# Four graph layers on one core: the tile pools' waits go from "all users of the space" to "users of the tile's own bytes"

## The chip, the cores and the metric

The kernel runs on one core of a Trainium2 chip. A core has five engines that each work off their own queue in order: TensorE (PE, with its weight loads shown as PEld), VectorE (DVE), ScalarE (ACT), GpSimd (POOL) and SyncE (SP, which here only starts transfers). They meet through semaphores: an instruction carries a list of waits and starts when all are met. Transfers run on 16 DMA engines and are started from the queues of SP, ACT and POOL. The metric is the device time of one execution in microseconds (us); less is better.

## The reference

A batch of N = 4096 nodes with D = 128 features and a dense adjacency matrix `adj` of 4096 by 4096 in float32 (64 MB). `adj` holds zeros and ones, is symmetric, and has ones on its diagonal. Four layers follow each other, each as `x = layernorm(x + layer(x, adj))`:

```python
# layer 0: hyperbolic GNN; pairwise weights times log maps
adj_att = adj * jax.nn.sigmoid((x_tangent @ wl)[:, None] + (x_tangent @ wr)[None, :] + att_b[0])
support_t = jnp.einsum('ij,ijd->id', adj_att, x_local)      # x_local[i, j] = logmap(h_i, h_j)
out = proj(expmap0(proj(expmap(h, support_t))))
# layer 1: transformer convolution, 4 heads of 32
e = jnp.where(mask[None], 0.0, jnp.exp(neg - m))            # mask = (adj == 0)
out = jnp.einsum('hnm,mhc->hnc', e / denom, v)              # then a learned gate against x @ Ws + bs
# layer 2: graph convolution with adj + I, normalised by degree
out = jax.nn.relu((d[:, None] * (adj + I) * d[None, :]) @ x @ weight)
# layer 3: additive attention over the neighbours
e = leaky_relu(A * s + A * r.T, 0.2)
out = softmax(where(A > 0, e, NEG), axis=1) @ (X @ W.T + b)
```

## The kernel before, in words

`tile_kernel` runs the program twice in source, once on the chip. First comes the class `Fast`, which relies on properties of the inputs (zeros and ones, symmetry, small scores) and checks them as it goes. It leaves flags in `good`. Only if a flag is bad does the class `Net`, from which `Fast` inherits, run again in full under `tc.If(again > 0)`. With these inputs it does not run, so the profile shows `Fast` alone.

`Fast` works in blocks of 512 by 512 (8 by 8 blocks of `adj`), each made of 4 tiles of 128 rows.

- **Layer 0, preparation** (0 to 75 us): the node vectors, norms and row constants. Its pools are closed by `pre_pools.close()`.
- **Layer 0, `pair_loop`** (75 to 646 us): 36 pairs of blocks (I, J) with I not above J, in an order written out by hand. For each pair PE makes the products `pz` (L1775 and L1778), ACT the sigmoids `w` (L1792) and the logarithms and exponentials, DVE the products, and PE the sums `pi` (L1859) and `pj` (L1874), which DVE adds into `X` (L1888). SP loads the float32 blocks `ad` and the row constants `di` and `dj`; POOL loads `el` and `er` and writes a bfloat16 copy of every block, `adjb`, to DRAM.
- **Layer 0, `mirror`** (646 to 745 us): a check that `adjb` is symmetric. SP loads 36 blocks `low` (L1683) and 28 blocks `up` (L1686), 512 KB each, into three buffers of each kind. PE multiplies them by the small matrices `sized` (made on DVE, L1677) and adds 12 steps into one PSUM tile `pm` (L1692, L1697; two buffers). DVE reduces each such sum to one column of flags, `odd` (L1702). In the same stretch DVE, ACT and POOL compute the end of layer 0: the `junk` sums (L537 and L541) and what follows to L604.
- **Layer 1, start** (745 to 790 us): ACT's queue loads the first block for the attention, `at0` (L2166). PE transposes `X` (L163), ACT and DVE copy the transposes out (L178), PE makes queries and keys (`pqk`, L2201), ACT and DVE cut them into two parts `cut` (L2203, L2204), SP stores these to DRAM as `qk` (L2210), and POOL loads them from there stacked by head, as `KS` and `QS` (L2181). Values (L2216) and `x @ Ws + bs` (L2226) follow on PE.
- **Layer 1, `attention_unshifted`** (790 to 1590 us): scores on PE (`ps`, L1994), exponentials on ACT (L2001, after a table load), mask on DVE (`e`, L2003), sums over neighbours on PE (`pv`, L2020). Beside it ACT's queue loads rows of `adj` (`nat`, L1970) and ACT sums them to degrees (L1976). SP loads the blocks `at` (L1959). At the end DVE normalises `X` (L2078, then L2094).
- **`layers23`** (1590 to 2048 us): layer 2 splits the features `Y` into three bfloat16 parts (ACT L2353, DVE L2355) and multiplies them by the blocks from `ring` on PE (`pa`, L2372). Meanwhile SP loads rows of `adj` (`nat`, L2331) that DVE looks through for values other than zero and one (L2336). Layer 3 follows in `attend_factored` (DVE L1570, PE L1573).

Pools are opened and closed by stage: `tc.tile_pool(name=..., bufs=...)` takes a stretch of SBUF or PSUM, and a later stage's pool lies on bytes that an earlier one gave back. The first tile in such reused bytes has to wait for their earlier users. By default a pool does that as a whole: its first tile waits for all the users of the closed pools that it lies on, in lists of up to some 18 semaphores. The order within each engine comes from the order in the source, and in parts from a list written out by hand (`pair_loop`).

Of the kernel before, what the change touches and what calls it, by code (L numbers as in the profile page):

```python
# [9 lines left out]
F32 = mybir.dt.float32  # L10
F32R = mybir.dt.float32r
BF16 = mybir.dt.bfloat16
# [3 lines left out]
PSUM = bass.MemoryType.PSUM  # L16

P = 128
# [43 lines left out]
class Net:  # L62
# [30 lines left out]

    def copies(self):
        self.adjT = self.dram.tile([self.NS, self.NS, P, 4, S], F32, tag="adjT", name="adjT")

    def pools(self, ctx, adj, big, t, o):

        self.on_scalar = 4
        if adj:  # L100
            self.adjp = ctx.enter_context(self.tc.tile_pool(name="adjp", bufs=adj))
        if big:
            self.ps_big = ctx.enter_context(self.tc.tile_pool(name="ps_big", bufs=big, space=PSUM))
        self.ps_t = ctx.enter_context(self.tc.tile_pool(name="ps_t", bufs=t, space=PSUM))
        self.ps_o = ctx.enter_context(self.tc.tile_pool(name="ps_o", bufs=o, space=PSUM))
# [202 lines left out]
    def layer0(self, x, weight, bias, att_w, att_b):  # L308
# [4 lines left out]
        with ExitStack() as ctx:  # L313
            self.on_scalar = 4
            keep = ctx.enter_context(tc.tile_pool(name="keep0", bufs=1))
            self.cols = ctx.enter_context(tc.tile_pool(name="cols0", bufs=1))
            adp = ctx.enter_context(tc.tile_pool(name="ad0", bufs=2))
            pre_pools = ctx.enter_context(ExitStack())
            pre = pre_pools.enter_context(tc.tile_pool(name="pre0", bufs=2))
            self.ps_t = pre_pools.enter_context(tc.tile_pool(name="ps_t", bufs=6, space=PSUM))  # L320
            one = pre_pools.enter_context(tc.tile_pool(name="one0", bufs=1))
            self.wide = pre_pools.enter_context(tc.tile_pool(name="wide", bufs=1))
            ps_c = pre_pools.enter_context(tc.tile_pool(name="ps_c", bufs=1, space=PSUM))
# [187 lines left out]
            late = ctx.enter_context(tc.tile_pool(name="late0", bufs=1))  # L511
            rot = ctx.enter_context(tc.tile_pool(name="rot0", bufs=6))
# [92 lines left out]
    def pair_loop(self, HT, HA, dr, rows, adp, early, rows4):  # L605
# [7 lines left out]
        with ExitStack() as ctx:  # L613
            atp = ctx.enter_context(tc.tile_pool(name="at0", bufs=2))
            wtp = ctx.enter_context(tc.tile_pool(name="sg0", bufs=6))
            wk = ctx.enter_context(tc.tile_pool(name="wk0", bufs=2))
            ps_t = ctx.enter_context(tc.tile_pool(name="ps_t0", bufs=2, space=PSUM))
            ps_z = ctx.enter_context(tc.tile_pool(name="ps_z0", bufs=2, space=PSUM))
            ps_i = ctx.enter_context(tc.tile_pool(name="ps_i0", bufs=1, space=PSUM))
            ps_j = ctx.enter_context(tc.tile_pool(name="ps_j0", bufs=1, space=PSUM))  # L620
# [224 lines left out]
    def layer1(self, Wq, bq, Wk, bk, Wv, bv, Ws, bs, Wb, R):  # L845
# [6 lines left out]
        with ExitStack() as ctx:  # L852
            self.on_scalar = 4
            keep = ctx.enter_context(tc.tile_pool(name="keep1", bufs=1))
# [27 lines left out]
            with ExitStack() as pctx:  # L882
                pre = pctx.enter_context(tc.tile_pool(name="pre1", bufs=1))
                rot = pctx.enter_context(tc.tile_pool(name="rot1", bufs=2))
                self.ps_t = pctx.enter_context(tc.tile_pool(name="ps_t", bufs=8, space=PSUM))
# [59 lines left out]
    def attention_unshifted(self, VA, KS, QS, at0, stack, R, wb):  # L945
# [4 lines left out]
        with ExitStack() as ctx:  # L950
            rot = ctx.enter_context(tc.tile_pool(name="rotf", bufs=1))
            natp = ctx.enter_context(tc.tile_pool(name="natf", bufs=2))
            atp = ctx.enter_context(tc.tile_pool(name="atf", bufs=1))
            ep = ctx.enter_context(tc.tile_pool(name="ef", bufs=3))
            ps_s = ctx.enter_context(tc.tile_pool(name="ps_s", bufs=3, space=PSUM))
            ps_v = ctx.enter_context(tc.tile_pool(name="ps_v", bufs=1, space=PSUM))
# [198 lines left out]
    def attention_shifted(self, V, qk, R, wb, spare):  # L1155
# [4 lines left out]
        with ExitStack() as ctx:  # L1160
            self.pools(ctx, 1, 2, 3, 1)
            self.wide = ctx.enter_context(tc.tile_pool(name="wide", bufs=2))
            keep = ctx.enter_context(tc.tile_pool(name="keeps", bufs=1))
            self.cols = ctx.enter_context(tc.tile_pool(name="cols1", bufs=1))
# [12 lines left out]
            work = ctx.enter_context(tc.tile_pool(name="work1", bufs=1))  # L1177
# [98 lines left out]
    def layers23(self, w2, weight, bias, a_s, a_r, out, Y):  # L1276
# [6 lines left out]
        with ExitStack() as ctx:  # L1283
            RING = 8
            ring = ctx.enter_context(tc.tile_pool(name="ring", bufs=1)).tile([P, RING, 4, S], F32, tag="ring", name="ring")
            keep = ctx.enter_context(tc.tile_pool(name="keep3", bufs=1))
# [10 lines left out]
            pre = pctx.enter_context(tc.tile_pool(name="pre3", bufs=1))  # L1297
            rot = pctx.enter_context(tc.tile_pool(name="rot2", bufs=2))
            wp = pctx.enter_context(tc.tile_pool(name="w2", bufs=4))
            ps_b = pctx.enter_context(tc.tile_pool(name="ps_b", bufs=2, space=PSUM))  # L1300
            ps_t = pctx.enter_context(tc.tile_pool(name="ps_t", bufs=2, space=PSUM))
            ps_s = pctx.enter_context(tc.tile_pool(name="ps_s", bufs=2, space=PSUM))
            ps_a = pctx.enter_context(tc.tile_pool(name="ps_a", bufs=2, space=PSUM))
# [228 lines left out]
    def attend_factored(self, F, XB, rho, col, wx, tot, eps, a0, ring, out):  # L1532
        nc, tc, N, NT, NS, D, X = self.nc, self.tc, self.N, self.NT, self.NS, self.D, self.X
        with ExitStack() as ctx:
            rot = ctx.enter_context(tc.tile_pool(name="rot3", bufs=2))
            RING = ring.shape[1]
            wp = ctx.enter_context(tc.tile_pool(name="w3", bufs=4))
            ps_a = ctx.enter_context(tc.tile_pool(name="ps_a3", bufs=2, space=PSUM))
            ps_b = ctx.enter_context(tc.tile_pool(name="ps_b3", bufs=2, space=PSUM))
# [43 lines left out]
    def attend(self, H, Rb, ring, weight, br, a_s, a_r, out):  # L1583
        nc, tc, N, NT, D, X = self.nc, self.tc, self.N, self.NT, self.D, self.X
        with ExitStack() as ctx:
            self.pools(ctx, 0, 0, 6, 2)
            self.wide = ctx.enter_context(tc.tile_pool(name="wide", bufs=2))
            one = ctx.enter_context(tc.tile_pool(name="one3", bufs=1))
            self.cols = ctx.enter_context(tc.tile_pool(name="cols3", bufs=1))
# [4 lines left out]
            with tc.tile_pool(name="pre3", bufs=1) as pre:  # L1594
# [15 lines left out]
            work = ctx.enter_context(tc.tile_pool(name="work3", bufs=1))  # L1610
# [33 lines left out]
class Fast(Net):  # L1644

    MARKS = 112

# [16 lines left out]
    def mirror(self, ctx):  # L1664
# [3 lines left out]
        keep = ctx.enter_context(tc.tile_pool(name="mir", bufs=1))  # L1668
        rot = ctx.enter_context(tc.tile_pool(name="mirt", bufs=3))
        ps = ctx.enter_context(tc.tile_pool(name="mirp", bufs=2, space=PSUM))  # L1670
# [38 lines left out]
    def pair_loop(self, HT, HA, dr, rows, adp, early, rows4):  # L1709
# [7 lines left out]
        with ExitStack() as ctx:  # L1717
            wtp = ctx.enter_context(tc.tile_pool(name="sg0", bufs=6))
            wk = ctx.enter_context(tc.tile_pool(name="wk0", bufs=2))
            ps_z = ctx.enter_context(tc.tile_pool(name="ps_z0", bufs=4, space=PSUM))  # L1720
            ps_i = ctx.enter_context(tc.tile_pool(name="ps_i0", bufs=1, space=PSUM))
            ps_j = ctx.enter_context(tc.tile_pool(name="ps_j0", bufs=1, space=PSUM))
# [218 lines left out]
    def attention_unshifted(self, VA, KS, QS, at0, stack, R, wb):  # L1941
# [4 lines left out]
        with ExitStack() as ctx:  # L1946
            rot = ctx.enter_context(tc.tile_pool(name="rotf", bufs=1))
            natp = ctx.enter_context(tc.tile_pool(name="natf", bufs=2))
            atp = ctx.enter_context(tc.tile_pool(name="atf", bufs=1))
            ep = ctx.enter_context(tc.tile_pool(name="ef", bufs=3))  # L1950
            ps_s = ctx.enter_context(tc.tile_pool(name="ps_s", bufs=3, space=PSUM))
            ps_v = ctx.enter_context(tc.tile_pool(name="ps_v", bufs=1, space=PSUM))
# [197 lines left out]
    def layer1(self, Wq, bq, Wk, bk, Wv, bv, Ws, bs, Wb, R):  # L2150
# [6 lines left out]
        with ExitStack() as ctx:  # L2157
            self.on_scalar = 4
            keep = ctx.enter_context(tc.tile_pool(name="keep1", bufs=1))
# [26 lines left out]
            with ExitStack() as pctx:  # L2186
                pre = pctx.enter_context(tc.tile_pool(name="pre1", bufs=1))
                rot = pctx.enter_context(tc.tile_pool(name="rot1", bufs=2))
                self.ps_t = pctx.enter_context(tc.tile_pool(name="ps_t", bufs=8, space=PSUM))
# [55 lines left out]
    def layers23(self, w2, weight, bias, a_s, a_r, out, Y):  # L2245
# [6 lines left out]
        with ExitStack() as ctx:  # L2252
            RING = 8
            ring = ctx.enter_context(tc.tile_pool(name="ring", bufs=1)).tile([P, RING, 4, S], BF16, tag="ring", name="ring")
            keep = ctx.enter_context(tc.tile_pool(name="keep3", bufs=1))
# [9 lines left out]
            pre = pctx.enter_context(tc.tile_pool(name="pre3", bufs=1))  # L2265
            rot = pctx.enter_context(tc.tile_pool(name="rot2", bufs=2))
            wp = pctx.enter_context(tc.tile_pool(name="w2", bufs=4))
            ps_b = pctx.enter_context(tc.tile_pool(name="ps_b", bufs=2, space=PSUM))
            ps_t = pctx.enter_context(tc.tile_pool(name="ps_t", bufs=2, space=PSUM))
            ps_s = pctx.enter_context(tc.tile_pool(name="ps_s", bufs=2, space=PSUM))  # L2270
            ps_a = pctx.enter_context(tc.tile_pool(name="ps_a", bufs=2, space=PSUM))
            parts = [pre.tile([P, NT, D], BF16, tag=f"Y{k}", name=f"Y{k}") for k in range(3)]
            identb = pre.tile([P, P], BF16, tag="identb", name="identb")
            nc.vector.tensor_copy(identb, self.ident)
            w = self.load_mat(w2, "w2")
            br = self.load_row(bias, "br3", keep)
            wn = self.load_mat(weight, "wn3", pre)
# [301 lines left out]
```

## Time and profile before

| | before |
|---|---|
| time, median of 3 runs | 2050.09 us (2048.27 to 2053.14) |
| profiled execution | 2050.21 us |
| its span in the profile | 2048.4 us |
| mean granted TensorE clock | 0.954 of full speed |
| busy: PE, DVE, ACT, POOL | 1900.9, 1736.6, 1328.8, 171.4 us |
| moved by DMA | 350.22 MB, mean 171 GB/s |

The span runs from the first to the last instruction of the profiled execution; 1.8 us lie around it. Busy times are sums over the whole span: an engine with a high sum can still be waiting at the start of a stage. The chain in the profile is the work that ended last, followed back from the end, at each step to what released it. Line numbers (L1683) are those of the kernel before.

### The profile page before, as it was taken

Reading aid. Unit: us, or ns where it says so; the run is one execution under the profiler, and the core shown is the slowest. Engines: PE = TensorE matmul, PEld = TensorE weight load, DVE = VectorE, ACT = ScalarE, POOL = GpSimd, SP = SyncE. Lnnn points to the kernel's source line nnn. Section 1 sums busy time; section 2 is a strip of 40 time slices with the busy share of each in tenths; the row PEclk is TensorE's granted clock in tenths of the full one; section 3 lists DMA queues with packets and bytes.
Section 4 is the critical chain, followed back from the end, with each engine's and each line's share of the span. In section 5 each row is a group of like instructions: output and inputs, shape, how many; then the busy total and the mean of one; then the engine's idle time right before and its main releaser. Section 6 shows DMA issues by size and latency. Waiting matters only on the chain.

```text
span 2048.4 us, 23818 instructions
## 1 busy us (share of the span) xinstructions
PE 1900.9 (93%) x8648; PEld 978.9 (48%) x8680; DVE 1736.6 (85%) x2685; ACT 1328.8 (65%) x1681; POOL 171.4 (8%) x269
## 2 busy tenths in 40 slices
PE   4789999999997788999999999999999799999997
PEld 4257766666666454333333333333333344444443
DVE  6579999998988946789999999999999777778986
ACT  5589999999997723777787777778787322210000
POOL 2211112111100221300000000000000000000000
PEclk8569999999999998999999999999999999999999
DMA  3488989899825977853535453545343799934441
GB/s 101 49 139 147 155 167 157 155 163 168 144 93 191 363 277 223 199 152 132 144 124 146 136 150 134 144 133 155 124 139 118 290 396 373 340 116 156 155 148 43
DMA packets 138064, 350.22 MB, mean 171 GB/s; under 512 B 13196, under 2 KB 56364, under 8 KB 125648
## 3 DMA queue, kind: packets, MB, share of 16 engines
q1 hardware_dynamic: 82944, 230.27, 32.3%
q0 software_dynamic: 45632, 50.69, 20.1%
q10 hardware_dynamic: 9360, 67.64, 9.9%
q8 instruction: 70, 1.15, 0.2%
q14 instruction: 58, 0.48, 0.1%
HBM read 371.54 MB, written 44.12 MB: 203 GB/s over the span
## 4 chain that ended last, share of the span: by engine, by line
PE 49%; DVE 24%; ACT 16%; DMA 6%; issue 4%; SPq 0%; POOL 0%; another core or an unknown queue 0%; ACTq 0%; DVEq 0%; POOLq 0%
PE pv L2020 11%; PE pa L1573 9%; DVE e L2003 9%; PE pa L2372 7%; PE ps L1994 6%; ACT e L2001 4%; PE pz L1775 3%; DMA up<-adjb 3%; DVE nat L1985 2%; ACT w L1792 2%; PE pi L1859 2%; PE pj L1874 2%; ACT s L1815 2%; ACT y L1811 2%; ACT y L1807 1%
## 5 line engine op out<-in xcount | busy, mean ns | idle before, releaser
L2003 DVE SCALAR_TENSOR_TENSOR e<-at,e 128x2048 f32<-128x2048 bf16 x256 | 582.6, 2286 | 77.3 <-ACT e L2001 76.7
L2001 ACT ACTIVATE e<-ps 128x1024 f32<-128x1024 f32 x512 | 492.9, 1024 | 150.6 <-PE ps L1994 121.6
L2020 PE MATMUL pv<-e,VA 128*64 128x512 f32 x2048 | 497.6, 607 | 6.7 <-DVE e L2003 5.7
L1994 PE MATMUL ps<-QS,KS 128*128 128x512 f32 x1024 | 314.8, 425 | 9.1 <-ACT e L2001 8.5
L1994 PEld LDWEIGHTS ps<-QS,KS 128*128 128x128 f32 x1024 | 170.9, 189 | 236.5 <-ACT e L2001 177.4
L2020 PEld LDWEIGHTS pv<-e,VA 128*64 128x64 f32 x2048 | 125.1, 136 | 250.2 <-issue 214.4
L1573 PE MATMUL pa<-w,Y 128*128 128x512 f32 x448 | 195.3, 594 | 0.0
L1775 PE MATMUL pz<-HT 128*128 128x512 f32 x288 | 171.8, 681 | 15.0 <-DVE w L1847 10.2
L1570 DVE SCALAR_TENSOR_TENSOR w<-rho,col,ring 128x512 f32<-128x512 f32 x224 | 162.7, 746 | 22.3 <-PE pa L1573 9.7
L2372 PE MATMUL pa<-ring,Y 128*128 128x512 bf16 x750 | 172.7, 384 | 8.7 <-ACT Y L2353 6.7
L1859 PE MATMUL pi<-HA,w 128*128 128x129 f32 x1152 | 156.6, 286 | 6.5 <-ACT s L1815 5.3
L1859 PEld LDWEIGHTS pi<-HA,w 128*128 128x128 f32 x1152 | 143.3, 199 | 18.2 <-issue 10.2
L1573 PEld LDWEIGHTS pa<-w,Y 128*128 128x128 f32 x448 | 83.8, 190 | 105.9 <-issue 80.3
L1976 ACT ACTIVATE nat<-nat 128x2048 f32<-128x2048 f32 x64 | 122.6, 1915 | 2.8 <-DMA nat<-in_adj_dram 2.8
L1874 PE MATMUL pj<-HA,w 128*128 128x129 f32 x896 | 120.7, 293 | 3.4 <-DVE X L1888 2.4
L2372 PEld LDWEIGHTS <-Y 128*128 128x128 bf16 x768 | 75.4, 99 | 100.9 <-ACT Y L2353 9.7
L1784 DVE TENSOR_SCALAR t<-pz 128x512 f32<-128x512 f32 x144 | 93.6, 682 | 30.2 <-PE pz L1778 30.2
L1874 PEld LDWEIGHTS pj<-HA,w 128*128 128x128 f32 x896 | 112.8, 205 | 11.2 <-issue 6.8
L1823 DVE SCALAR_TENSOR_TENSOR t<-t,s 128x2048 f32<-128x2048 f32 x36 | 82.3, 2286 | 13.4 <-ACT s L1815 13.4
L1792 ACT ACTIVATE w<-di,dr 128x512 f32<-128x512 f32 x144 | 90.6, 707 | 1.5 <-DMA di<-rows 1.5
L2336 DVE SCALAR_TENSOR_TENSOR nat<-nat 128x2048 f32<-128x2048 f32 x32 | 73.1, 2287 | 20.5 <-DMA nat<-in_adj_dram 20.5
L1847 DVE TENSOR_TENSOR w<-w,ptz 128x512 f32<-128x512 f32 x112 | 73.4, 681 | 18.7 <-PE ptz L1842 17.3
(410 smaller groups left out, 2343.1 us busy)
## 6 DMA issues: line engine op xcount, KB each, us to landing
nat<-in_adj_dram ACTq DMA_DIRECT2D x64, 1024.0 KB, 5.1
ring<-adjb SPq DMA_DIRECT2D x128, 512.0 KB, 4.7
ad<-in_adj_dram SPq DMA_DIRECT2D x36, 1024.0 KB, 9.4
adjb<-in_adj_dram POOLq DMA_DIRECT2D x64, 512.0 KB, 11.4
nat<-in_adj_dram SPq DMA_DIRECT2D x32, 1024.0 KB, 7.5
at<-adjb SPq DMA_DIRECT2D x63, 512.0 KB, 3.5
low<-adjb SPq DMA_DIRECT2D x36, 512.0 KB, 5.1
up<-adjb SPq DMA_DIRECT2D x28, 512.0 KB, 6.6
```

The lines of the kernel that those rows point to most:

```text
L1570: nc.vector.scalar_tensor_tensor(w, rho[:, I * S : (I + 1) * S], col[:, 0, j : j + 1], at[:, jb, :], op0=ALU.max, op1=ALU.mult)
L1573: nc.tensor.matmul(pa, lhsT=F[:, j, :], rhs=w, start=False, stop=(j == NT - 1), skip_group_check=True)
L1775: nc.tensor.matmul(pz, lhsT=HT[:, j * P : (j + 1) * P], rhs=HT[:, I * S : (I + 1) * S], start=True, stop=False)
L1792: nc.scalar.activation(w[:, jb, :], st[p]["d"][k], AF.Sigmoid, bias=dr[:, 4 * J + jb : 4 * J + jb + 1])
L1859: nc.tensor.matmul(row[I, "po"][ib // 2][:, ib % 2, :], lhsT=st[p]["w0"][:, jb, ib * P : (ib + 1) * P], rhs=HA[:, 4 * J + jb, :], start=False,
L1874: nc.tensor.matmul(pj[:, a, :], lhsT=st[p]["w1"][:, ib, jb * P : (jb + 1) * P], rhs=HA[:, 4 * I + ib, :], start=(ib == 0), stop=(ib == 3),)
L1976: nc.scalar.activation(nat, nat, AF.Identity, accum_out=self.deg2[:, k, i : i + 1])
L1994: nc.tensor.matmul(p[:, h, :], lhsT=KS[:, h2 + h, jb * P : (jb + 1) * P], rhs=QS[I % 2][:, h2 + h, :], start=True, stop=True,)
L2001: nc.scalar.activation(e[:, h2 : h2 + 2, :], p, AF.Exp)
L2003: nc.vector.scalar_tensor_tensor(e, at[:, jb % 4, :].unsqueeze(1).to_broadcast([P, NH, S]), 0.0, e, op0=ALU.not_equal, op1=ALU.mult,)
L2020: nc.tensor.matmul(st["po"][h // 2][g : g + 64, :], lhsT=VA[:, o : o + 64], rhs=e[:, h, :], start=(jb == 0), stop=(jb == NT - 1), skip_gro ...
L2372: nc.tensor.matmul(st["pa"], lhsT=parts[k][:, j, :], rhs=at[:, jb, :], start=(I > 0 and j == k == 0), stop=(j == NT - 1 and k == 2), skip_ ...
```

## The change

`Net` gets a method that opens a pool with a given kind of wait, and nearly all pools of `Net` and `Fast` are opened by it. `Net` keeps the kind "pool", which is the default that was there before. `Fast` sets "tile": a tile in reused bytes waits only for the instructions that used its own bytes. The pools of the constructor, and two pools in `tile_kernel` (the flags, and `Y`), stay as they were.

```diff
+    waits = "pool"
+
+    def pool(self, **kw):
+        return self.tc.tile_pool(reuse_waits=self.waits, **kw)
+
     def copies(self):
...
@@ Fast
+    waits = "tile"
+
...
     def mirror(self, ctx):
...
-        keep = ctx.enter_context(tc.tile_pool(name="mir", bufs=1))
-        rot = ctx.enter_context(tc.tile_pool(name="mirt", bufs=3))
-        ps = ctx.enter_context(tc.tile_pool(name="mirp", bufs=2, space=PSUM))
+        keep = ctx.enter_context(self.pool(name="mir", bufs=1))
+        rot = ctx.enter_context(self.pool(name="mirt", bufs=3))
+        ps = ctx.enter_context(self.pool(name="mirp", bufs=2, space=PSUM))
...
     def pair_loop(self, HT, HA, dr, rows, adp, early, rows4):
...
-            ps_z = ctx.enter_context(tc.tile_pool(name="ps_z0", bufs=4, space=PSUM))
+            ps_z = ctx.enter_context(self.pool(name="ps_z0", bufs=4, space=PSUM))
...
-            natp = ctx.enter_context(tc.tile_pool(name="natf", bufs=2))
+            natp = ctx.enter_context(self.pool(name="natf", bufs=2))
...
-            keep = ctx.enter_context(tc.tile_pool(name="keep1", bufs=1))
+            keep = ctx.enter_context(self.pool(name="keep1", bufs=1))
...
-            rot = pctx.enter_context(tc.tile_pool(name="rot2", bufs=2))
+            rot = pctx.enter_context(self.pool(name="rot2", bufs=2))
```

The other pools are changed in the same way. No instruction's work changes, and the instructions stand in the same order on every engine. What differs is which semaphores some of them wait for.

## The prediction

> **What bounds the kernel now.** I read the page first, for what the whole is made of, and then the stage boundaries, because the change touches only where pools open, and pools open between stages.
>
> ```profile
> span 2048.4 us, 23818 instructions
> PE 1900.9 (93%) x8648; PEld 978.9 (48%) x8680; DVE 1736.6 (85%) x2685; ACT 1328.8 (65%) x1681; POOL 171.4 (8%) x269
> PE 49%; DVE 24%; ACT 16%; DMA 6%; issue 4%; SPq 0%; POOL 0%; another core or an unknown queue 0%; ACTq 0%; DVEq 0%; POOLq 0%
> ```
>
> PE is busy for 93% of the span. Inside the stages the end is set by PE with DVE, and the change alters no instruction there. The gain can only lie in the other 7%. The chain gives DMA 6%, which is some 120 us, and most of that is one stage: `mirror`, from 646 to 745 us, where every step of the chain is a transfer of `up` or `low`. The windows show how it begins (columns: window, length, busy time and count of PE, PEld, DVE, ACT, POOL, granted TensorE clock, DMA share, GB/s):
>
> ```profile
> 641.00:646.00 5.00, 4.97 (x38) 4.31 (x36) 0.48 (x2) 0.00 (x0) 0.00 (x0) 1.00 0.00 0
> 646.00:650.00 4.00, 0.28 (x1) 0.09 (x1) 3.99 (x34) 1.57 (x10) 0.00 (x0) 1.00 0.74 266
> 650.00:655.00 5.00, 4.06 (x32) 2.80 (x33) 5.00 (x42) 4.77 (x33) 0.00 (x0) 0.66 1.02 404
> 730.00:735.00 5.00, 3.22 (x38) 2.45 (x38) 0.69 (x1) 0.00 (x0) 0.00 (x0) 1.00 0.71 237
> ```
>
> For five microseconds before a stage that lives on transfers, nothing is transferred. From 650 the 16 DMA engines are full. The timeline says what the first transfer and the first matmul of the stage waited for (start, duration, engine, line, what, and in brackets the idle time before it with its releaser):
>
> ```profile
> 639.19 1.95 PE L1874 MATMUL pj<-HA,w 128*128 128x129 f32 x16
> 646.00 0.32 SPq L1683 DMA_DIRECT2D low<-adjb  x1
> 649.72 0.38 PE L1692 MATMUL pm<-low,sized 128*128 128x512 bf16 x1 [3.74 <-DVE sized L1677]
> 715.34 0.68 DVE L1702 TENSOR_REDUCE odd<-pm 128x1 f32<-128x512 f32 x1
> 719.39 0.69 DVE L1702 TENSOR_REDUCE odd<-pm 128x1 f32<-128x512 f32 x1 [0.26 <-PE pm L1697]
> 744.88 0.35 ACTq L2166 DMA_DIRECT2D at<-adjb  x1
> 791.63 0.36 ACTq L1970 DMA_DIRECT2D nat<-in_adj_dram  x1
> 792.02 1.28 ACT L2001 ACT_TABLE_LOAD   x1 [15.89 <-PE ps L1994]
> ```
>
> And the chain at two other boundaries:
>
> ```profile
> 744.84 0.70 DVE odd L1702
> 745.54 0.14 issue
> 745.67 3.69 PE pt L163 x32
> ...
> 1604.89 0.61 DVE X L2094 x2
> 1605.63 5.08 DMA nat<-in_adj_dram
> 1610.94 2.30 DVE nat L2336 x2
> ```
>
> **The change part by part.** The order of instructions is the same on all five engines in both programs; only wait lists differ. So I followed every changed wait to the instruction that ends it and took that one's time from the trace. Most of the waits dropped had ended long before their instruction was reached: ACT's first table load of the pair loop loses seven of eight waits, but it has 3.0 us of slack. Such edits cost and give nothing, because the engine's own preceding instruction covers them. Six boundaries are left.
>
> 1. Start of the pair loop. The first `pz` matmul (L1775, at 75.90) waited for DVE at 75.86; its own bytes are free when ACT's copy L178 ends at 75.38. PE is free at 74.97. Up to 0.48 us, and PE paces the loop's first blocks: I take 0.4.
>
> 2. Start of mirror. The first `low` load waited for the last `pi` matmul of the pair loop (645.99). Now it waits for the last `pj` matmul (641.15), and the five loads queued behind it on SP have waits long past. That is 4.84 us earlier, into idle DMA engines. The data of the first pair then land near 644.6, and what is late next is DVE: it makes `sized` from 647.03, after `X` at 646.01, so the first mirror matmul goes from 649.72 to about 647.3. The loads keep their lead of 4.84, as each block takes 1.25 to 1.29 us on full DMA engines and PE needs only some 1.76 per pair of blocks; six buffers hold the surplus. Two things take part of it back. First, the reduces L1702 stand in DVE's queue within layer 0's tail: the seventh starts at 715.34 whatever PE does, and the ninth accumulation needs its PSUM tile. PE ended the eighth at about 719.37 (the row at 719.39), so not more than 3.36 us fits there (719.37 less 716.01, the seventh's end). The stall of 1.5 us (4.84 less 3.36) is partly covered by the loads that wait in buffers (about 0.9), so I take 0.6 off. Second, point 3. 4.84 less 0.6 is 4.24.
>
> 3. The `at0` load (L2166, ACT's queue) may now go at 730.28, not 744.81. It is 512 KB in the last part of mirror, where the DMA share is 0.71 and the `low` loads are on the chain. The trace's own rule is 1.27 us for each 512 KB when the engines are full. [...] Were the queue separate, the load would be free and mirror would give 4.24; by the rule with full engines it would give 2.97. At a share of 0.71 part fits into gaps; I take 0.9 off. Mirror then gives 3.3. Its ends: 1.5 (another slip at the PSUM tile or a full extra block), and 4.84; with the landing gap before the fourth `low` block gone (3.1 instead of 1.25) 1.9 more.
>
> 4. Transposes (L163). They waited for DVE's last reduce at 745.54, and now for the one before it, long past. PE is free at 744.86 and started at 745.67: 0.81 us. The fifth group needs the last reduce's tile, but reaches it after it is free. POOL's fill of VA still waits for PE and lies beside.
>
> 5. Start of attention. ACT's queue had the `nat` load L1970 in front, which waited for the last landing of `qk` (791.25), and the table load of the exponential came behind it at 792.02. The new wait is for PE's last L2226 (788.20). The table load is then bounded by the scores, which end near 790.63: 1.35 us earlier, and with it the first exponential on the chain. The landing of `qk` is late next, needed by the second tile at about 795.2, with 4 us of slack; SP's `at` loads go 3.4 us earlier, ahead of nothing on the chain. Bounds 0.5 (the `nat` load, 1 MB now first, delays the last `qk` tile) and 1.35; I take 1.35, as the row has the slack.
>
> 6. Start of layer 2. SP's first wide `nat` load waited for the last `X` normalisation (L2094, 1605.50). It now waits for an earlier one (L2078, 1602.84): 2.66 us. DVE idles 4.07 us for this load, and the `Y` split it has left to do ends at 1606.87, so the lead is not cut before about 1608.3. PE's first `pa` follows, and PE is 99% busy from 1628 to the end. I take 2.65; bounds 1.5 (the second load still waits for 1605.5) and 3.9.
>
> [...]
>
> ```profile
> 1610.94 2.29 DVE L2336 SCALAR_TENSOR_TENSOR nat<-nat 128x2048 f32<-128x2048 f32 x1 [4.07 <-DMA nat<-in_adj_dram]
> 1614.55 0.61 PE L2372 MATMUL pa<-ring,Y 128*128 128x512 bf16 x1 [4.42 <-ACT Y L2353]
> ```
>
> PE idles 4.42 here and 3.74 at mirror's start, and the granted clock then is 0.66 (650 to 655; 1610 to 1620). [...] By the trace it is worth nothing: mirror is paced by transfers and layer 2's start by the ACT and DVE split. I take 0 and let 1.7 into the range.
>
> Sum: 0.4 + 3.3 + 0.8 + 1.35 + 2.65 = 8.5 us. The profiled execution took 2050.21 (span 2048.4 and 1.8 around it), 0.12 over the median of 2050.09. So 2050.1 less 8.5 is 2041.6.
>
> Added waits: some loads of `low`, `up`, KS, QS and `at` get one to four more, each on an event past before the load is reached. Bound 0 to a few hundredths each, on queues that have slack: 0.
>
> **The rivals.** R1, the early transfers collide. `low`, `at0` and `nat` move forward, but the end of mirror is set by the latency of its last diagonal blocks (share 0.67 to 0.71 there) and by DVE's in-order tail, so mirror gives nothing. For it: the cap of 3.36 and the shared engines. Against it: the share of 0.92 to 1.02 from 646 to 730. Left are 0.4 + 0.8 + 1.35 + 2.65 = 5.2, or 2.8 with the last two at their low ends: 2044.9 to 2047.3.
>
> R2, the change does almost nothing: each freed instruction finds the next thing late at the same moment (`sized` for mirror, the score for ACT, `Y` for layer 2). For it: most changed waits are of this kind. Against it: the DMA engines are idle at 641 to 646 and the rows above name the dropped waits' enders as the last. 2048 to 2050.
>
> R3, slower: the pair loop's start shifts by 0.48 us, and with it the order in which POOL's `adjb` copies (11.4 us from issue to landing) and SP's `di` and `dj` loads meet on the DMA engines. Loads of `di` or `dj` stand on the chain at 160.68, 220.89, 311.42 and 354.84, with 6 to 10 us each. One slip behind a 1 MB source read costs 2.5 us at 400 GB/s. Four such slips (10 us) outweigh the 8.5: about 2051.6. It decides from the fourth slip on. Against it: a shift of half a microsecond is small against the loop's 15.8 us per block pair (570 us for 36), and can as well go the other way.
>
> **How the numbers follow.** The forecast 0.72, R1 0.18, R2 0.07, R3 0.03. A measurement of this kernel can tell about 0.2% from no change, which is 4.1 us; the limit is 2046.0. Faster takes the forecast and most of R1 (0.11): 0.83. The rest of R1 and R2 are the same: 0.14. R3 is 0.03. The likeliest case alone spans 2037 (4.84 + 1.9 at mirror, 3.9 at layer 2, all else full: 13.2) to 2045.5; with R1 the range is 2037.0 to 2047.0, and R2, R3 and R1's tail stay out.
>
> **What would show it.** Counted from the pair loop's last matmul: the first `low` load 4.8 us before it, the first `pm` about 1.3 us after it rather than 3.7, mirror's last matmul about 95.5 rather than 98.8 later, and the transposes directly behind that. `at0` goes out before 731. The table load follows the first scores directly. DVE's first L2336 has an idle time near 1.4, not 4.07. I am wrong if the time from the last `pi` to the first transpose does not shrink, if the ninth accumulation waits for L1702 by more than 1.5 us, if DVE waits for `qk` in attention's second tile, or if the pair loop's own length moves by more than 1 us.

## The result, and the profile after

The changed kernel takes 2036.8 us (median of 6 runs, 2034.63 to 2038.32), the kernel before 2048.03 (6 runs, 2043.14 to 2053.14). The ratio is 0.994, with a 95% interval from 0.9922 to 0.9957, so about 12 us are gained. Forecast were 2041.6 and a gain of 8.5, in a range from 2037.0 to 2047.0: the direction was right, the size too small, and the result lies 0.2 us under the range. Line numbers of the changed kernel are 5 or 6 higher than those of before (L1683 is now L1689), and up to 3 more in versions with added lines. One slow execution of the kernel of experiment 5, 3694.82 us, is left out of its ratio; its cause is not known.

The page, of the changed kernel:

```profile
span 2033.4 us, 23810 instructions
PE 1881.0 (93%) x8648; PEld 971.7 (48%) x8680; DVE 1737.1 (85%) x2685; ACT 1328.4 (65%) x1681; POOL 171.8 (8%) x269
PE 52%; DVE 25%; ACT 13%; DMA 6%; issue 4%; SPq 0%; another core or an unknown queue 0%; POOL 0%; ACTq 0%; DVEq 0%; POOLq 0%
```

The same work is done, but PE is busy for 19.9 us less. No instruction got smaller, and the mean granted clock is 0.964, not 0.954, so PE ran at a higher clock somewhere. The place is the first 60 us of the pair loop. Windows of the kernel before (window, length, busy time and count of PE, PEld, DVE, ACT, POOL, granted TensorE clock, DMA share, GB/s):

```profile
75.00:80.00 5.00, 4.10 (x5) 1.29 (x5) 0.98 (x2) 0.52 (x2) 0.38 (x1) 0.50 0.27 73
80.00:95.00 15.00, 15.00 (x18) 4.23 (x17) 3.46 (x5) 11.11 (x10) 5.93 (x10) 0.50 1.12 104
95.00:110.00 15.00, 15.00 (x18) 4.42 (x17) 6.83 (x8) 11.28 (x6) 1.01 (x2) 0.50 0.28 38
```

and of the changed kernel:

```profile
75.00:80.00 5.00, 4.55 (x9) 1.46 (x8) 1.49 (x3) 0.71 (x2) 0.60 (x1) 0.77 0.10 22
80.00:95.00 15.00, 14.27 (x30) 4.49 (x28) 6.21 (x8) 12.72 (x11) 6.17 (x11) 1.00 1.19 125
95.00:110.00 15.00, 5.19 (x16) 3.55 (x17) 11.80 (x9) 14.87 (x9) 2.10 (x4) 0.59 1.01 209
```

The start of the loop, first before, then after (in brackets PE's idle time ahead and what ended it):

```profile
75.90 2.08 PE L1775 MATMUL pz<-HT 128*128 128x512 f32 x2 [0.93 <-DVE e L494]
75.60 1.94 PE L1781 MATMUL pz<-HT 128*128 128x512 f32 x2 [0.45 <-ACT rows L183]
77.89 1.13 PE L1781 MATMUL pz<-HT 128*128 128x512 f32 x2
```

Before, PE was busy without a break from 80 to 110 us at half clock, and it set the pace. Now the granted clock is 1.00 from 77.28 to 97.75 us. By 94.28 it has finished the `pz` work that took it to 108.70 before, and then ACT sets the pace (14.87 of 15 us busy). In these two profiles the pair loop ends at 637.77, not 645.99.

The other boundaries, in the timeline of the changed kernel:

```profile
632.96 0.32 SPq L1689 DMA_DIRECT2D low<-adjb  x1
639.16 0.39 PE L1698 MATMUL pm<-low,sized 128*128 128x512 bf16 x1 [1.40 <-DVE sized L1683]
717.41 0.35 ACTq L2172 DMA_DIRECT2D at<-adjb  x1
724.66 0.61 PE L1698 MATMUL pm<-low,sized 128*128 128x512 bf16 x1 [4.11 <-DMA low<-adjb]
736.43 3.66 PE L168 MATMUL pt<-ident,X 128*128 128x128 f32 x32
781.37 1.28 ACT L2007 ACT_TABLE_LOAD   x1 [14.14 <-PE ps L2000]
1596.76 2.29 DVE L2342 SCALAR_TENSOR_TENSOR nat<-nat 128x2048 f32<-128x2048 f32 x1 [2.16 <-DMA nat<-in_adj_dram]
1600.37 0.39 PE L2378 MATMUL pa<-ring,Y 128*128 128x512 bf16 x1 [2.09 <-ACT Y L2359]
```

The first `low` load leaves 4.81 us ahead of the pair loop's end, and mirror's first matmul comes 1.39 us after that end, both as forecast; the idle time ahead of it is 1.40 us. But mirror's last matmul ends at 736.60, which is 98.83 us after the pair loop. It was 98.82 before: the lead was lost again inside mirror, and the row at 724.66 shows where.

### The profile page after: what moved, and what is told of

Its sections match the earlier page's. It is cut to its first block, busy times and chain, and to the rows that moved or that the text cites. A ratio compares the mean times of both kernels' runs of the same rounds, so it can differ in the third digit from the quotient of the medians.

```text
span 2033.4 us, 23810 instructions
## 1 busy us (share of the span) xinstructions
PE 1881.0 (93%) x8648; PEld 971.7 (48%) x8680; DVE 1737.1 (85%) x2685; ACT 1328.4 (65%) x1681; POOL 171.8 (8%) x269
## 4 chain that ended last, share of the span: by engine, by line
PE 52%; DVE 25%; ACT 13%; DMA 6%; issue 4%; SPq 0%; another core or an unknown queue 0%; POOL 0%; ACTq 0%; DVEq 0%; POOLq 0%
PE pv L2026 11%; PE pa L1578 10%; DVE e L2009 9%; PE pa L2378 7%; PE ps L2000 6%; ACT e L2007 4%; PE pj L1880 3%; PE pi L1865 3%; PE pz L1781 3%; DVE nat L1991 2%; DMA up<-adjb 2%; ACT w L1798 2%; DVE t L1829 2%; ACT nat L1982 1%; PE ptz L1848 1%
## 5 line engine op out<-in xcount | busy, mean ns | idle before, releaser
L2378 PE MATMUL pa<-ring,Y 128*128 128x512 bf16 x750 | 172.0, 383 | 7.4 <-ACT Y L2359 5.1
L1781 PE MATMUL pz<-HT 128*128 128x512 f32 x288 | 160.8, 641 | 18.5 <-DVE w L1853 10.0
L2378 PEld LDWEIGHTS <-Y 128*128 128x128 bf16 x768 | 75.5, 99 | 98.9 <-issue 8.2
```

The source lines that it names most:

```text
L1781: nc.tensor.matmul(pz, lhsT=HT[:, j * P : (j + 1) * P], rhs=HT[:, I * S : (I + 1) * S], start=True, stop=False)
L2378: nc.tensor.matmul(st["pa"], lhsT=parts[k][:, j, :], rhs=at[:, jb, :], start=(I > 0 and j == k == 0), stop=(j == NT - 1 and k == 2), skip_ ...
```

## The experiments

The pools' kinds of wait can be set stage by stage, so each boundary could be changed alone. In the edits `own` stands for a pool with waits by tile and `tc.tile_pool` for one with the waits of before. Ratios are to the kernel before on the same chip. Executions of one kernel spread by 10 us and more here, so the ratios are read with their intervals, and stages are read from the profiles by the distance between two landmarks.

**1. The pair loop alone, and all but the pair loop.** Is the gain there caused by the change, or by the spread?

```diff
 # pair_only: everything else waits as before
-            ps_z = ctx.enter_context(tc.tile_pool(name="ps_z0", bufs=4, space=PSUM))   # and the other four
+            ps_z = ctx.enter_context(own(name="ps_z0", bufs=4, space=PSUM))
 # no_pair: the changed kernel with
-            ps_z = ctx.enter_context(own(name="ps_z0", bufs=4, space=PSUM))            # and the other four
+            ps_z = ctx.enter_context(tc.tile_pool(name="ps_z0", bufs=4, space=PSUM))
```

> Only the five pools of the pair loop wait by tile, all others wait as before. Theory A (clock): the first pz starts some 0.45 us earlier, the gap ahead of it on PE halves, and the granted TensorE clock rises within the first pz instead of staying at 0.50 until about 130 us; the pair loop ends 4 to 9 us earlier and the whole takes 4 to 9 us less than the kernel before, with mirror and layer 2 as long as before. Rival B (spread): the clock of the pair loop's start differs from execution to execution whatever the waits; the whole is within 1 us of the kernel before.

> The changed kernel, but the pair loop's five pools wait for the whole pool as before. Theory A (clock): the granted clock is 0.50 from 75 to about 130 us again, and the kernel is 4 to 9 us slower than the changed one: about 2041 to 2045 where before is 2048. Rival B (spread): no difference from the changed kernel, 2036 to 2038.

Pair loop alone: 0.9977 (0.9963 to 0.9991), or 4.7 us less; its profile has the full clock at 80 us. All but the pair loop: 0.9962 (0.9949 to 0.9975), or 7.8 us less, with this in its windows:

```profile
75.00:80.00 5.00, 4.07 (x8) 1.48 (x6) 0.81 (x2) 0.99 (x3) 0.00 (x0) 0.50 0.22 59
80.00:95.00 15.00, 15.00 (x17) 3.92 (x15) 3.63 (x6) 10.40 (x9) 6.33 (x10) 0.50 1.06 103
```

The half clock is back with the old waits of these five pools. The two parts add to 12.5 us, about what the whole change gives. The pair loop alone decides against the spread, as its interval leaves 1 us out. The version without it does not by itself: its interval overlaps the changed kernel's.

**2. Is it the clock, or the earlier start?** The kernel before, with all its waits, and PE's gap ahead of the first `pz` filled with work that nobody reads.

```diff
             nc.tensor.transpose(p[0 : 3 * NT, 0, :], de.rearrange("p k t -> p (k t)"), self.ident)
+            warm = self.ps_t.tile([P, 4, P], F32, tag="pt", name="warm")
+            for k in range(4):
+                nc.tensor.transpose(warm[:, k % 4, :], self.ident, self.ident)
```

> The kernel before, with all its waits, and four extra 128 by 128 transposes on PE ahead of the pair loop (about 1 us), which fill PE's gap ahead of the first pz; the first pz is not earlier. Theory A (clock, by PE's activity in the gap): the granted clock rises during the first pz as in the changed kernel, the pair loop ends 4 to 9 us earlier and the whole takes 4 to 9 us less than before. Rival A2 (it is the time of the start, or the wait list itself, not the activity): 0.50 until about 130 us, the whole within 1 us of before or up to 1 us slower.

0.9962 (0.995 to 0.9975), or 7.8 us less. Its timeline:

```profile
74.61 1.06 PE L499 MATMUL warm<-ident 128*128 128x128 f32 x4
75.83 1.47 PE L1784 MATMUL pz<-HT 128*128 128x512 f32 x2 [0.17 <-DVE e L502]
77.66 1.13 PE L1784 MATMUL pz<-HT 128*128 128x512 f32 x2
```

The first `pz` still waits for DVE and starts no earlier than before (75.90). Only the gap is smaller, 0.17 us, and the clock rises within that first `pz` (0.84 from 75 to 80 us, 1.00 from 80 to 95): two matmuls take 1.47 and then 1.13 us, where the kernel before took 2.08 each time. So a gain of this size comes without an earlier start and without any changed wait. The freed 0.48 us matters for the gap that it closes, not for the time it saves. How much of this version's gain is the clock's, the end of experiment 3 shows.

**3. What does the clock answer to?** Three more versions of the kernel before. In the first, 14 transposes stand further ahead and the gap of 0.93 us stays; in the other two, 8 or 28 transposes stand in the middle of the `pz` work.

```diff
 # warm_early: ahead of the row transposes (L478)
+            for k in range(14):
+                nc.tensor.transpose(warm[:, k % 4, :], self.ident, self.ident)
 # warm_in, warm_in28: in distance(), for the first block pair, ahead of the third pz
+                if (p, b) == (0, 2):
+                    for k in range(8):                                   # 28
+                        nc.tensor.transpose(pz[:, k % 4 * P : (k % 4 + 1) * P], self.ident, self.ident)
```

> The kernel before, with all its waits, and 14 extra transposes on PE (some 3.6 us) that fill PE's idle time of 4 us ahead of the row transposes at 72 us; the gap of 0.93 us ahead of the first pz stays. Theory A (a stretch of dense work lifts the clock, wherever it lies, and the pz work then holds it): the granted clock is 1.00 by 75 us and stays there through the 0.93 us gap; 5 to 9 us less than before. Rival A3 (the gap ahead of the first pz itself is what keeps the clock down): 0.50 again from 76 us until 115 us or later, and no gain.

> The kernel before, with all its waits, and 8 extra transposes (some 2 us at half clock) on PE between the second and the third pz of the first block pair, into the tile that the third pz then overwrites; PE is busy without a gap ahead of them and behind them. Theory A (pz work at half clock does not count as enough, denser work does): the clock rises to 1.00 at about 82 to 85 us instead of 115 or later; 3 to 7 us less than before. Rival A3 (only the start of the loop counts): 0.50 until 115 us or later, and up to 2 us more than before.

> [...] Theory A (a long enough stretch of dense work lifts the clock; the pz work alone at half clock does not): the clock rises to 1.00 within the transposes, at 80 to 86 us, and the pz work behind holds it. Rival A4 (once the loop has begun at half clock, no work on PE lifts it before the loop's first pause): 0.50 until 115 us or later, and some 5 us more than before at the end of the first pz's.

With 8 transposes nothing rises: 0.50 until 120 us, 1.0009 (0.9995 to 1.0024). With 28 it does:

```profile
76.50 2.08 PE L1784 MATMUL pz<-HT 128*128 128x512 f32 x2 [0.93 <-DVE e L499]
79.23 6.02 PE L1783 MATMUL pz<-ident 128*128 128x128 f32 x28
85.08 1.02 PE L1784 MATMUL pz<-HT 128*128 128x512 f32 x2
86.46 1.12 PE L1784 MATMUL pz<-HT 128*128 128x512 f32 x2
```

PE is busy without a break from the first `pz` on, during these transposes and after them. In the kernel before, 35 us of `pz` work left the clock at 0.50; here it rose at the end of the 6.02 us of transposes (0.51 from 80 to 85 us, 1.00 from 85 to 90), and the `pz` work behind them ran at 1.00 until 105. The 6 us cost about what they bring: 0.9992 (0.998 to 1.0004).

The 14 early transposes missed their forecast. In its profile the two `pz` matmuls at 77.39 take 1.12 us, so the clock is full from the first `pz` behind a gap of 0.93 us (1.00 from 80 to 95), but the transposes delay PE's next work by 1.5 us and the pair loop ends no earlier (646.70). The whole is slower, 1.0021 (1.0008 to 1.0034). The mean clocks of its 22 executions run from 0.949 to 0.964, so in part of them the clock was probably half again; no profile shows that.

The traces' clock records show in part how so short a gap decides, and where chance comes in. In all 14 profiles a stretch of one granted clock lasts a whole number of steps of 3.41 us (before, the half clock lasts 30 steps, from 32.16 to 134.56; after, 13 steps, from 32.90 to 77.28). One stretch at most, cut by the record's edge, is no multiple. In these profiles the clock changes on this grid alone. The step that holds the gap, first before, then after with the step behind it:

```profile
73.12:76.54 3.42, 2.49 (x10) 1.40 (x9) 0.29 (x1) 1.85 (x4) 0.00 (x0) 0.50 0.03 7
73.86:77.28 3.42, 2.97 (x9) 1.09 (x6) 0.29 (x1) 1.31 (x3) 0.00 (x0) 0.50 0.08 18
77.28:80.69 3.41, 3.41 (x8) 1.14 (x7) 1.38 (x2) 0.00 (x0) 1.29 (x3) 1.00 0.20 51
```

In the six profiles with the gap of 0.93 us and no early transposes, PE was busy for 2.5 us of that step, and the clock stayed at half. In the five with the gap of 0.45 us it was busy for 2.96 us; the clock rose behind four of these steps and not behind the fifth (changed kernel, second time). With the 14 early transposes the step ended at 76.91, inside the gap, with 2.93 us busy, and the clock rose. Steps filled by `pz` work alone, 3.41 us busy, did not lift it. So PE's busy time is not all that counts, and what else does stays open.

The end of the pair loop hides what the clock is worth. In six profiles at half clock the loop ended at 641.5 to 646.0 (mean 643.9), in seven at full clock at 636.1 to 646.7 (mean 640.5). An earlier landmark separates them, DVE's fifth copy of a `pj` sum into `X` (L1886). Before, after, and with the gap filled:

```profile
180.07 0.42 DVE L1886 COPY X<-pj 128x258 f32<-128x258 f32 x1
174.59 0.43 DVE L1892 COPY X<-pj 128x258 f32<-128x258 f32 x1 [0.47 <-PE pj L1880]
168.14 0.42 DVE L1895 COPY X<-pj 128x258 f32<-128x258 f32 x1
```

It comes at 178.3 to 180.7 us in the six at half clock, at 174.0 to 175.1 in five at full clock (the early transposes among them, with 174.7), and at 168.1 in the two that fill the gap with four transposes. So the full clock is worth some 5 us there, and the version with early transposes has that gain too and loses it later. The further 6 us of the filled gap are not the clock's. Most of them show on the chains, of the changed kernel and of the one with the gap filled:

```profile
118.09 11.29 DMA dj<-rows
129.41 5.01 ACT w L1798 x8
```

```profile
115.07 14.81 ACT w L1801 x24
```

Behind these rows the two are 4.5 us apart (134.42 and 129.88). In the five at full clock without that filling, ACT waits 2.6 to 4.6 us for a `dj` load that leaves at 117.1 to 118.5 and takes 11.3 to 13.3 us. In the two it leaves at 116.3, takes 5.8 to 5.9, and ACT does not wait. So part of the gain in experiment 2 comes from when loads leave and land, which nobody aimed at. What slows that load, and what spreads the loop's ends further on, is left open.

**4. Where mirror's lead went.** The changed kernel with the `at0` load held back, and with it on SP's queue behind the last `low` load; mirror's pools alone; and the changed kernel a second time.

```diff
 # at0_late
-            keep = ctx.enter_context(own(name="keep1", bufs=1))
+            keep = ctx.enter_context(tc.tile_pool(name="keep1", bufs=1))
 # at0_sync
-            nc.scalar.dma_start(out=at0, in_=self.block(0, 0))
+            nc.sync.dma_start(out=at0, in_=self.block(0, 0))
 # mirror_only: the kernel before with the pools mir, mirt, mirp, late0, rot0 by tile
+        rot = ctx.enter_context(own(name="mirt", bufs=3))
```

> The changed kernel, but the pool of at0, KS, VA and QS waits as before, so that the at0 load leaves after mirror's last matmul. Theory C (collision): the early at0 load delays the low block that lands with it by about 2.9 us, and the longer idle time lets PE's clock fall, 2 us more; without it mirror keeps its lead of 4.9 us to its end, and the whole is 3 to 5 us faster than the changed kernel: 2032 to 2034. Rival D (latency): mirror's last blocks are bound by the round trip of three buffers, and the lead is lost there anyway: within 1 us of the changed kernel.

> The changed kernel, but the at0 load is issued on SP's queue, in order behind mirror's last low load, not on ACT's. Theory C (collision): mirror takes 93 to 94 us from the pair loop's last matmul, as with the load held back, and the 512 KB fall into the transposes, when the DMA engines are idle, and not among the qk stores, which saves up to 1.3 us more: 4 to 6 us faster than the changed kernel. Rival D (mirror's last blocks are slow by their round trip anyway): within 1 us of the changed kernel.

> Only mirror's three pools and the two pools beside them (late0, rot0) wait by tile. Theory C: the first low load leaves some 4.8 us before the pair loop's last matmul, at0 leaves after mirror as before, and mirror keeps the lead: 93 to 94.5 us from the pair loop's last matmul; the whole 4 to 5 us less than before. The clock at the pair loop's start is 0.50 as before. Rival (DVE's queue): PE waits for the reduces, mirror takes 95 to 96 us, the whole 2 to 3 us less.

> The changed kernel again, to stand beside the others on one chip and to give a second profile. Theory (clock at the pair loop, collision at mirror's end): first pz at full clock by 80 us; the time from the pair loop's last matmul to mirror's last is 97 to 99 us again, as in the kernel before, because the at0 load lands among mirror's last blocks; whole 0.5 to 0.7% under the kernel before. Rival (the loss at mirror's end was an accident of one execution): 93 to 94 us.

| kernel | at0 leaves | pair loop's end to mirror's end, us | last 6 blocks and the end, us | ratio |
|---|---|---|---|---|
| before | after | 98.82 | 12.46 | |
| changed | among the last blocks | 98.83 | 17.36 | 0.994 |
| changed, second time | among the last blocks | 97.76 | 17.46 | 0.9947 (0.9927 to 0.9966) |
| all but the pair loop | among the last blocks | 97.49 | 17.63 | 0.9962 |
| at0 held back | after | 93.10 | 13.21 | 0.9925 (0.9899 to 0.9951) |
| mirror's pools alone | after | 94.41 | 13.89 | 0.9971 (0.9959 to 0.9983) |
| at0 on SP's queue | behind the last block | 96.56 | 14.59 | 0.9935 (0.9914 to 0.9956) |

The fourth column runs from the landing of the seventh block from the end to mirror's last matmul. Wherever `at0` leaves among the last blocks it is 17.4 to 17.6 us; in the other eleven profiles it lies between 12.5 and 15.2. Mirrors with the old waits scatter, from 96.5 to 101.1 us in seven profiles (mean 98.3), so the third column is read by groups: 97.5 to 98.8 with `at0` among the last blocks, 93.1 to 95.3 in the three profiles with mirror's pools by tile and `at0` after (experiment 6 is the third). The chain, first of the changed kernel:

```profile
715.25 2.13 another core or an unknown queue
717.39 7.22 DMA low<-adjb
729.59 4.46 DMA low<-adjb
```

and of the one with `at0` held back:

```profile
714.11 5.34 DMA up<-adjb
721.02 3.72 DMA low<-adjb
726.42 5.02 DMA low<-adjb
```

A `low` load on the chain left at 717.39 and `at0` at 717.41. They landed together, at 724.61 and 724.78, 7.2 and 7.4 us after issue. It was no accident of one execution: this block, the sixth from the end, took 6.6 to 7.2 us in the three profiles with `at0` beside it and 3.3 to 4.6 in the other eleven. PE idled 4.11 us for it, and its clock fell, to 0.50 from 722.39 to 729.22. The windows are of the changed kernel:

```profile
717.00:725.00 8.00, 3.24 (x36) 2.27 (x35) 0.69 (x1) 0.00 (x0) 0.00 (x0) 0.84 0.78 273
725.00:730.00 5.00, 4.78 (x38) 3.85 (x38) 0.00 (x0) 0.00 (x0) 0.00 (x0) 0.58 0.33 103
```

From 725 to 730, at 0.58, PE takes up to 0.63 us for a 128x512 matmul of L1698 that took 0.38 at full clock. SP, which has waited 3.7 us for that block, waits 3.0 more for PE's L1703 and sends its next `low` load at 727.6, 7.0 us after the last; the DMA engines are at 0.33, where the 8 us before had 0.78. The clock fell at this place, for 3.41 or 6.83 us, in all three profiles with the early `at0`; with `at0` held back it stays at 1.00 from 713 to 733. So the early `at0` takes back about all that the early `low` load won; how that divides between the load and the clock was not measured. The total does not decide it: the intervals of `at0` held back and of the changed kernel overlap. The version on SP's queue has no collision with `at0`, but mirror was 3.5 us longer than with `at0` held back, and its total can't be told from the changed kernel's either: its expectation was met by neither theory.

The second profile of the changed kernel held a surprise: half clock at the pair loop's start (0.50 from 75 to 110 us). Of its 15 executions 11 have a mean clock of 0.963 or more and take 2023.6 to 2041.3 us; four have 0.956 or less and take 2045.0 to 2049.7. The two profiled executions have 0.964 (full at the start) and 0.955 (half), so I take the 11 to be at full clock; that is inferred. The half microsecond makes the full clock likely, not certain. With the gap filled (experiment 2), all 18 executions have 0.960 or more; of the kernel before, 167 executions on four chips lie between 0.948 and 0.962, 15 of them at 0.960 or more.

**5. Layers 2 and 3 alone.**

```diff
 # l23_only: everything else waits as before
-            rot = pctx.enter_context(tc.tile_pool(name="rot2", bufs=2))    # and the other pools of layers23
+            rot = pctx.enter_context(own(name="rot2", bufs=2))
```

> Only the pools of layers 2 and 3 wait by tile. [...] Rival F (the load alone): 2.7 us less in this stage and the clock falls as before. Rival G: the Y split is late at the same moment, nothing is gained.

0.9992 (0.9975 to 1.0009): too small for the timing to tell. By the stage, from the end of the first exponential to the end of DVE's first look: 817.1 to 818.9 us in the seven profiles with layer 2's pools as before (mean 818.1), 815.0 to 817.3 in the seven with them by tile (mean 816.0). That is 2.1 us; my estimate was 4, from the load and a clock that stays at 1.00, and for the load alone 2.7 (F). On the clock, two rows, of this version and of the one without the pair loop:

```profile
1610.89 0.39 PE L2378 MATMUL pa<-ring,Y 128*128 128x512 bf16 x1 [1.57 <-ACT Y L2359]
```

```profile
1604.60 0.61 PE L2378 MATMUL pa<-ring,Y 128*128 128x512 bf16 x1 [3.51 <-ACT Y L2359]
```

A `pa` matmul took 0.39 us at full clock (changed kernel, 1600.37, at 1.00) and 0.61 at half (before, 1614.55, at 0.50). In eight profiles the gap ahead of this `pa` is 3.51 to 4.45 us, and in each the clock fell, within the gap or at most 1.2 us behind it. In the other six it is 1.46 to 2.26 us; the clock held in four and fell in two (0.5 us behind a gap of 2.20, 2.0 us behind one of 2.26). Yet from DVE's look to layer 2's last `pa` (L2378) it is 176.1 to 176.3 us in all 14 profiles, whether the clock fell or not: the clock there is worth nothing to that end.

**6. The best of both.** The changed kernel with `at0` held back (as in 4) and the four transposes (as in 2).

> The changed kernel with the at0 load held back behind mirror (its pool waits as before) and four extra transposes ahead of the pair loop. Theory (clock and collision): every execution has the full clock from 80 us, so the slow quarter of the changed kernel's executions (2045 and above) is gone; mirror takes 93 to 94 us; 0.75 to 0.9% under the kernel before, about 2031 to 2034. Rival: the clock and the lead of mirror are eaten later (pair loop bound by its transfers): like the changed kernel, 0.5 to 0.6%.

2030.01 us, 0.9904 (0.9878 to 0.993) of the kernel before on its chip: 20 us less. Its pair loop has the full clock, the mean clock is 0.960 or more in all six executions, and mirror takes 95.31 us, more than the 93 to 94 expected. That is the lowest ratio of all versions; its interval overlaps that of `at0` held back alone.

## Why the prediction was right or wrong

| step of the sum | forecast, us | measured, us | from |
|---|---|---|---|
| pair loop's start | 0.4 (0 to 0.48) | 4.7 (1.8 to 7.6) | pair loop alone; some 5 by the fifth copy of `pj` |
| mirror's lead without at0 | 4.24 | 4.0 | mean of 3 profiles with at0 after (94.3) against 7 of unchanged mirrors (98.3) |
| at0 among the last blocks | -0.9 | -3.8 | mean of 3 profiles (98.0) |
| transposes | 0.8 | 0.8 | chain: L168 begins at 736.59, where the last L1703 ends |
| start of attention | 1.35 | 2.4 | last L2226 to the end of the first exponential: mean 7.1 in 8 profiles with the old waits, 4.7 in 6 with the new |
| layer 2 | 2.65 | 2.1 | experiment 5 |
| clock after the long gaps | 0 | 0 | experiment 5 |
| sum | 8.5 | 10.2 | |

**Pair loop.** The prediction took the 0.48 us at their length and added that PE paces the loop's first blocks. That was the place to ask why PE was the pace. The windows of before showed it, at 0.50 from 50 us on; I had read the granted clock only at the two boundaries where PE idles long, and had ruled that the gain can only lie in PE's idle 7%. The step that failed is the term "I take 0.4": the gain is not a start that moves but a clock that rises, and it measured 4.7 us. Idle time and the clock do go together elsewhere in these profiles: in experiment 5 the clock fell at all eight gaps of 3.51 to 4.45 us, but also behind two of the six shorter ones (2.20 and 2.26 us). Work on PE did not by itself bring it back: PE was busy for 35 us here, as the profile counts it, and the clock stayed at 0.50. That the full clock came in the profiled execution at all was luck in part, as the second profile shows.

**R3**, the slower case, started from the same shift of the pair loop's phase. The shift did matter, by ten times its length, and to the other side. The slip that R3 named is there too, in the `dj` load that ACT waits for, but the clock outweighs it.

**Mirror.** Start, first matmul and the lead held as forecast to the last blocks. The cap by DVE's reduces did not bind in this profile: the wait for L1708 ahead of the ninth accumulation was 0.94 us (up to 2.43 in the version without the pair loop and 2.30 with `at0` held back, so elsewhere it did), and the lead stood at 4.9 us up to the seventh block from the end. The term that failed is the 0.9 for `at0`. It was sized as bandwidth (1.27 us for 512 KB, some of it in gaps), but at that point the chain runs through the round trip of one `low` load, 3.3 to 4.6 us without `at0`. A second load at the same moment raised that to 6.6 to 7.2 us, and the clock fell at the longer idle time (4.11 us in the changed kernel); together they cost 3.8. R1 named this collision and its result for mirror, nothing gained; its total was missed because of the pair loop. (The share of 0.92 to 1.02 that stood against R1 is not so over the whole stretch from 646 to 730: it is 0.74 up to 650 and 0.86 from 725.) One of the prediction's own signs of being wrong came true: the pair loop's length moved by 7.9 us between the two profiles. Another nearly did: the time from its last `pi` to the first transpose shrank by 1.0 us, which is the transposes' own step.

**Transposes, attention, layer 2.** The transposes came as forecast and layer 2 0.55 us short. Attention gave 1.05 more than forecast, beyond its upper bound: the profile of before, from which it was sized, has the shortest stretch of the eight (6.15 against a mean of 7.1). R2 is refuted by each of them. No run shows the 1.7 us let into the range for the clock after the two long gaps (4.42 and 3.74 us): in layer 2 the clock was worth nothing (176.1 to 176.3 us from DVE's look to the last `pa`, whether it fell or not), and what it was worth at mirror's start was not measured.

The sum of the measured steps, 10.2, lies within the interval of the whole (8.8 to 16 us). What it leaves open, about 2 us, is less than the spread of the pair loop's end.

## What to carry to other kernels

When a freed wait is sized, look at the granted clock on both sides of the gap that it closes, not only at the gap: if PE sets the pace at half clock, closing part of a gap can be worth more than its length (0.48 us freed, 4.7 us gained here). A few transposes into an unread tile test this, but look where in the stage the gain arrives: here about half of it came from loads that landed at a better moment. And a load that is freed to leave early was not free here, where it met a stretch that waits for the round trip of other loads (`at0`: 3.8 us lost, 0.9 forecast): size it there by latency, not by bandwidth, and hold it back if nobody needs it yet.

## What the runs showed of the hardware

- PE busy without a break did not by itself lift the clock: `pz` work (two matmuls of 128 by 512 in float32, then one with 4 rows) ran 35 us at 0.50. 8 transposes (1.97 us) in its midst changed nothing (0.50 until 120 us); 28, or 6.02 us, did (1.00 from 85 us), and after that the same `pz` work ran at 1.00 until 105 us. Why it held the clock but did not lift it was not settled.
- The granted clock changed only on a grid of 3.41 us in these 14 profiles. A gap of 0.93 us at the pair loop's start left it at half in six of seven profiles, one of 0.45 us in one of five.
- Two loads of 512 KB issued 0.02 us apart took 7.2 and 7.4 us; the block concerned took 3.3 to 4.6 us in the eleven profiles without the second load.
